# When ScalarE's tables are called up: tiny unread activations where stages begin, and two edits in the mixtures of experts

## The chip, the cores and the metric

The kernel is one program on one core of a Trainium2 chip. Its time is the device time of one execution in microseconds (us); the time of a version is the median of several executions. A profile shows one execution in detail: the span from its first to its last instruction, the instructions of each engine, and what they waited for. The engines are PE (TensorE, the matrix engine; PEld is its loading of weights), DVE (VectorE), ACT (ScalarE), POOL (GpSimd) and SP (SyncE, which here issues most DMA transfers).

## What is computed

Four layers of a Perceiver: 512 tokens of 256 channels (8 sequences of 64) against a context of 8 times 1601 rows of 128 channels. Each layer adds three blocks to the residual `x`: attention to the context, attention or a recurrence over the tokens, and a feed-forward block, which in each of the layers is a mixture of experts.

```python
x = x + _L0_xattn_ref(_layernorm(x, axis=-1), ctx_512, ...)
x = x + _L0_attn_ref(_layernorm(x, axis=-1), ...)
x = x + _L0_ffn_ref(_layernorm(x, axis=-1), ...)
...
x = x + _L3_ffn_ref(_layernorm(x, axis=-1), ...)
```

The parts that matter here are where exponentials and other non-linear functions are taken: softmax (Exp) in all the attentions, `gelu(..., approximate=False)` in the two blocks of layer 0's cross-attention, `silu` in the mixtures of layers 0, 2 and 3, the tanh form of `gelu` in that of layer 1, and in two places of the mixtures:

```python
# layer 0: two of 8 experts, their shares
top_logits, idx = jax.lax.top_k(router, K)
probs = jax.nn.softmax(top_logits.astype(jnp.float32), axis=-1).astype(x.dtype)
...
# layer 3: two of 16 experts, and a shared one behind a gate
shared = shared * jax.nn.sigmoid(x @ shared_gate_w.T)
logits = x @ gate_w.T
probs = jax.nn.softmax(logits.astype(jnp.float32), axis=-1)
rw, sel = jax.lax.top_k(probs, TOP_K)
rw = rw / rw.sum(axis=-1, keepdims=True)
```

## The kernel before

**Layout.** Everything is in 32-bit floats on 128 partitions. The 512 tokens are four tiles of 128 (`NI` = 4); the residual `X` stays on chip throughout. The stages follow one another in program order, each with its own pools of on-chip buffers. By the trace: a1 and m1 (self-attention of layer 0's cross block and its feed-forward) up to about 120 us; a2 (attention to the context, 16 heads of 32) about 120 to 567; m2 to 610; b0 (attention over tokens) to 663; f0 (first mixture) to 775; x1 (context attention) to 828; r1 (recurrence) to 868; f1 (second mixture) to 971; x2 (context attention, heads of 64) to about 1410; b2 to 1475; f2 (third mixture) to 1560; x3 (context attention, 16 heads of 16, "narrow") to about 1850; b3 to 1923; f3 (fourth mixture) to the end.

**What sets the order.** Each engine works through its own queue strictly in order and waits there on semaphores. Inside `tc.manual_schedule(...)` blocks (`flash` of x1, `turned_attention` of a2, x2 and x3, m1's feed-forward, and the loops over experts) the order of the named engines is the order in which the program is written. Outside of them a scheduler orders each engine's instructions from estimated times: what is ready first goes first, and of what is ready, what is written first. `tc.keep_in_program_order(...)` pins one instruction behind whatever was traced before it on its engine. All waits are placed by the framework. ScalarE's functions come from tables; the framework puts an instruction `ACT_TABLE_LOAD` ahead of an activation whose function is not in the tables that are loaded at that point of ACT's final order.

**The context attentions.** In a2, x2 and x3 `turned_attention` runs 7 steps for each of 16 halves (a sequence and half of its heads). A step makes scores of 256 context rows on PE into `psS` (L883; x3: L1006), copies them out on ACT into `raw` (L884; x3: L1011), keeps a running maximum on DVE (`top`, L799 and L805), subtracts the maximum nine to ten steps later on DVE (`raw`, L826), takes Exp on ACT (L830), and sums values on PE (`psav`, L895; x3: L1025). The score buffers are two (x3: one large one), so PE's next scores wait for ACT's copies. In x1 `flash` works on 8 half tiles: scores (L1710), their maximum on DVE (L683 to L688, `nm`), Exp on ACT (`P`, L696), transposes (`psp`, L710), sums (L1716).

**The mixtures.** A routing chain of small operations on DVE (`top2`, `chosen`, `deal`: lines 1108 to 1228) finds each token's two experts and its place. Indirect DMAs on POOL (L1217) then deal the rows out in that order, SP reads them back (L1239), and a hand-ordered loop runs the experts' tiles. Meanwhile PE makes the shared expert's halves in `up(c)` (L1144), whose Silu is on ACT (`sg`, L1147) and whose product is on DVE (`hT`, L1148). In f3, `softmax_e` (lines 1091 to 1098) stands at the head of the routing chain: the maximum (`gm`), the subtraction (`sc`, L1092), Exp on ACT (L1093), the sum (`gs`, L1095) and the division. Its gate is the sigmoid of column 16 of the logits (L2098), read only by the sums at the end of the stage. In f0 the two shares need one Exp, `e2` (L1656), written after the last `up`, and three small DVE operations (`r` and `e2`, lines 1658 to 1660); they are read at the end of the stage by `collect`.

**Where stages begin.** m1, f0, x1, f1, x2 and others open with `keep_busy(ps, n)`: n matmuls on `ones` (L349) whose result nobody reads. `transposed` and `lin_T` then turn the normalised tokens and make queries; copies out of them alternate between ACT (L340) and DVE (L342) in `evac`. `turn_into` (L1330) is an Identity activation on ACT. `collect` (L1301) fetches half of the answered rows through a DMA queue of ACT's own.

Of the kernel before, what the change touches and what calls it, by code (L numbers as in the profile page):

```python
# [11 lines left out]
F32 = mybir.dt.float32  # L12
AF = mybir.ActivationFunctionType
# [260 lines left out]
def perceiver(ctx: ExitStack, tc: tile.TileContext, d, col_at, row_at, const_at, out):  # L274
# [46 lines left out]
    def chunks(w, n):  # L321
        return w.rearrange("p (k n) -> p k n", n=n)
# [14 lines left out]
    def evac(dst, src):  # L337
        turn[0] ^= 1
        if turn[0]:
            nc.scalar.copy(dst, src)  # L340
        else:
            nc.vector.tensor_copy(dst, src)  # L342

    def keep_busy(ps, n):

# [1004 lines left out]
    with tc.tile_pool(name="l0res", bufs=1) as res, ExitStack() as both:  # L1350
# [82 lines left out]
        with general() as ps, tc.tile_pool(name="m1", bufs=1) as mp:  # L1433
# [30 lines left out]
            def turn2(i):  # L1464
                if i >= 0:
                    turn_into(ps, xT2, i, xn[:, i, :], ("a2lnx_g", "a2lnx_b"))

            keep_busy(ps, 8)
            staggered(norm1, enter1)
            with tc.manual_schedule(engines=FOUR):  # L1470
# [13 lines left out]
        with tc.tile_pool(name="a2o", bufs=1) as op:  # L1484

            qT = op.tile([P, 4, NT], F32, tag="qT", name="qT")
            with ExitStack() as _:
                wq, wk, wv, li1 = (weight("a2" + k) for k in ("wq", "wk", "wv", "li1"))
                wk3, wv3 = chunks(wk, CY), chunks(wv, P)
                with general() as ps:  # L1490
                    lin_T(ps, chunks(wq, 512), xT2, 512, lambda c, t: evac(qT[:, c, :], t))
                ps, psS, psO, fp = turned_pools("a2")
                with ps as ps, psS as psS, psO as psO, fp as fp:
# [55 lines left out]
                        psS, psO, fp, lambda b: qks[b].rearrange("p h s -> p (h s)"), lambda b: (cns[b], cts[b]), leave  # L1549
                    )  # L1550
                    turned_attention(ps, fp, *parts, hooks)
            with general() as ps, tc.tile_pool(name="m2", bufs=1) as mp:
                x3 = tpool.tile([P, C // P, NT], F32, tag="T", name="T")
                xn = nat.tile([P, NI, C], F32, tag="nat", name="xn")
                mvs2 = {}

                def scale2(i):
                    norm_by(xn[:, i, :], xo[:, i, :], mvs2[i])
                    nc.gpsimd.tensor_tensor(X[:, i, :], X[:, i, :], xo[:, i, :], ALU.add)

                def enter2(i):
                    turn_into(ps, x3, i, xn[:, i, :], ("a2ln3_g", "a2ln3_b"))

                def attended(i, t):
                    nc.vector.tensor_tensor(xo[:, i, :], t, xo[:, i, :], ALU.add)
                    mvs2[i] = norm_of(xo[:, i, :])
                    if i > 0:
                        scale2(i - 1)
                    if i > 1:
                        enter2(i - 2)  # L1570

                lin_nat(ps, chunks(li1, C), qT, attended)
                keep_busy(ps, 2)
                enter2(NI - 2)
                scale2(NI - 1)
                keep_busy(ps, 3)
                enter2(NI - 1)
                after_attention("a2", xo, x3, mp, ps, into_X, lambda: None)
# [60 lines left out]
    with general() as ps, tc.tile_pool(name="f0", bufs=2) as pool:  # L1639
# [5 lines left out]
        xT = transposed(ps, xn)  # L1645
        lg = logits(ps, pool, wg, xT)
        hots, (m1, m2) = top2(pool, lg, 8)
        sel = chosen(pool, hots, 8)
        up, down = gated_parts(ps, pool, xT, ws1, ws2, 704)
        up(0)  # L1650
        ofi, n = deal(ps, pool, dealts[0], xn, hots, sel, 8, W0)
        for c in range(1, 6):
            up(c)
        e2 = pool.tile([P, NI], F32, tag="e2", name="e2")
        nc.vector.tensor_tensor(e2, m2, m1, ALU.subtract)
        nc.scalar.activation(e2, e2, AF.Exp)  # L1656
        r = pool.tile([P, NI], F32, tag="pr", name="pr")
        nc.vector.tensor_scalar(r, e2, 1.0, None, ALU.add)
        nc.vector.reciprocal(r, r)
# [16 lines left out]
    with tc.tile_pool(name="x1", bufs=1) as pool:  # L1676
# [5 lines left out]
        qb = pool.tile([P, NI], F32, tag="qb", name="qb")  # L1682
        oT = pool.tile([P, NT], F32, tag="oT", name="oT")
        with general() as ps:
            keep_busy(ps, 7)
            xT = transposed(ps, normed(X))
            lin_T(ps, wq, xT, C, lambda c, t: nc.scalar.activation(qT[:, c, :], t, AF.Identity, bias=col("x1bq", c)))
            lin_T(ps, wk, qT, CY, lambda c, t: evac(qk, t))
            t = ps.tile([P, 512], F32, tag="ps", name="psb")
            for i in range(NI):  # L1690
                for k in range(2):
                    nc.tensor.matmul(t[:, i : i + 1], qT[:, k, i * P : (i + 1) * P], col("x1bk", k), start=k == 0, stop=k == 1)
            nc.vector.tensor_copy(qb, t[:, :NI])
# [142 lines left out]
    with general() as ps, tc.tile_pool(name="f1", bufs=2) as pool:  # L1836
# [3 lines left out]
        xn = normed(X)  # L1840
        xT = transposed(ps, xn)
        sc = softmax_e(pool, logits(ps, pool, wg, xT), 8)
        hots, _ = top2(pool, sc, 8)
        sel = pool.tile([P, NI, 8], F32, tag="sel", name="sel")
        nc.vector.tensor_tensor(sel, hots[0], hots[1], ALU.add)
# [74 lines left out]
    with tc.tile_pool(name="x2", bufs=1) as pool:  # L1920
# [2 lines left out]
        qT = pool.tile([P, 8, NT], F32, tag="qT", name="qT")  # L1923

        with general() as ps:
            keep_busy(ps, 2)
            xT = transposed(ps, normed(X))
            lin_T(ps, chunks(wq, 1024), xT, 1024, lambda c, t: evac(qT[:, c, :], t))
            add_row_to_X("x2o")
# [117 lines left out]
    with tc.tile_pool(name="x3", bufs=1) as pool:  # L2047
        wq, wkv, wo = (weight("x3" + k) for k in ("q", "kv", "o"))
        qT = pool.tile([P, 2, NT], F32, tag="qT", name="qT")
        oT = pool.tile([P, 2, NT], F32, tag="oTall", name="oTall")  # L2050
        with general() as ps:
            xT = transposed(ps, normed(X))
            lin_T(ps, chunks(wq, C), xT, C, lambda c, t: evac(qT[:, c, :], t))
        ps, psS, psO, fp = turned_pools("x3", 1, 1, 3)
# [20 lines left out]
    with general() as ps, tc.tile_pool(name="f3", bufs=2) as pool:  # L2075
# [3 lines left out]
        xT = transposed(ps, xn)  # L2079
        lg = logits(ps, pool, wg, xT)  # L2080
        sc = softmax_e(pool, lg[:, :, :16], 16)
        hots, (m1, m2) = top2(pool, sc, 16)
        sel = chosen(pool, hots, 16)
        up, down = gated_parts(ps, pool, xT, ws1, ws2, 704)
# [9 lines left out]
        for k, m in enumerate((m1, m2)):  # L2094
            shares.append(pool.tile([P, NI], F32, tag=f"share{k}", name="share"))
            nc.vector.tensor_tensor(shares[k], m, r, ALU.mult)
        gate = pool.tile([P, NI], F32, tag="gate", name="gate")
        nc.scalar.activation(gate, lg[:, :, 16], AF.Sigmoid)  # L2098

        def act(t, h, ys):  # L2100
            sg = pool.tile([P, P], F32, tag="sgd", name="sgd", bufs=2)
# [31 lines left out]
```

## Time and profile before

| what | us |
| --- | --- |
| three runs | 2009.70, 2011.72, 2015.39 |
| median | 2011.72 |
| the profiled execution | 2014.61 |
| its span, first to last instruction | 2012.8 |
| ACT busy in it | 1036.5 (1721 instructions) |
| mean granted clock of PE, as a share of full speed | 0.984 |

The profile's groups give, for a line, engine and operation, the tiles written and read, the count, the busy time, the mean time of one, and after the second bar the idle time of the engine just ahead of them with what ended it. The timeline gives the start and length of instructions in order of time, with the idle time ahead and its releaser in brackets. PE's instructions overlap, so an idle of PE is the time in which none ran. In the first page's slices of the span the granted clock of PE is printed in tenths; a table by stretches gives it as a share, with the busy time of each engine.

### The profile page before, as it was taken

What the parts mean: (1) busy time and instruction counts of PE and PEld (TensorE: products, weight loads), DVE (VectorE), ACT (ScalarE), POOL (GpSimd) and SP (SyncE); (2) the same over time, 40 slices, a digit from 0 to 9 for tenths busy, and PEclk for the clock granted to TensorE, in tenths of its full rate; (3) what the DMA queues carried; (4) which work ended last, traced back from release to release, by engine and by line L of the source; (5) the groups of instructions that cost most, each with busy time, mean ns of one, the idle gap of its engine ahead of it and who ended that gap; (6) DMA issues with size and microseconds to landing.
All of it is one profiled execution on the core that took longest, in us unless ns stands there. A gap on an engine that the chain in (4) does not pass through costs nothing.

```text
span 2012.8 us, 36872 instructions
## 1 busy us (share of the span) xinstructions
PE 1894.9 (94%) x15394; PEld 1411.5 (70%) x15394; DVE 1235.7 (61%) x2124; ACT 1036.5 (51%) x1721; POOL 270.0 (13%) x331
## 2 busy tenths in 40 slices
PE   8989999999999998989999999999999799998899
PEld 6656777777768576669567777778866577776757
DVE  6556676766726433661366666665544599999743
ACT  2347777777532222402265555654212599998323
POOL 3431010111012211000000000000122210100124
PEclk8999999999999999999999999999999899999999
DMA  9310000000005207318200100100421110100322
GB/s 312 117 63 1 18 18 18 18 28 1 1 26 221 89 27 270 118 62 277 100 17 34 34 34 34 35 18 17 183 82 61 48 35 19 36 19 17 143 76 98
DMA packets 38230, 142.29 MB, mean 71 GB/s; under 512 B 4936, under 2 KB 17872, under 8 KB 32496
## 3 DMA queue, kind: packets, MB, share of 16 engines
q1 hardware_dynamic: 32448, 127.98, 17.8%
q0 software_dynamic: 3696, 10.11, 1.4%
q8 instruction: 122, 2.00, 0.4%
q10 hardware_dynamic: 1920, 1.84, 0.3%
q14 instruction: 44, 0.36, 0.1%
HBM read 129.28 MB, written 19.71 MB: 74 GB/s over the span
## 4 chain that ended last, share of the span: by engine, by line
PE 64%; DVE 15%; ACT 9%; issue 2%; POOL 2%; DMA 2%; SPq 0%; DVEq 0%; ACTq 0%; POOLq 0%
PE psav L895 17%; PE psS L883 16%; PE psgd L1260 4%; DVE raw L826 4%; DVE top L805 4%; PE psl L412 2%; PE psn L421 2%; PE psy L1281 2%; ACT raw L1011 2%; ACT raw L830 1%; PE psh L1903 1%; PE psy L1907 1%; PE psg L1144 1%; PE psq L471 1%; ACT cn L1413 1%
## 5 line engine op out<-in xcount | busy, mean ns | idle before, releaser
L895 PEld LDWEIGHTS psav<-cn,raw 128*128 128x128 f32 (+1 forms) x3328 | 403.2, 192 | 87.6 <-issue 86.3
L826 DVE TENSOR_TENSOR raw<-raw,mb 128x1024 f32<-128x1024 f32 (+1 forms) x336 | 381.7, 1140 | 62.5 <-ACT mb L822 62.5
L895 PE MATMUL psav<-cn,raw 128*128 128x129 f32 (+1 forms) x3328 | 407.4, 275 | 0.7 <-ACT raw L830 0.7
L883 PE MATMUL psS<-qk,ct 128*128 128x512 f32 (+1 forms) x832 | 397.5, 600 | 8.3 <-ACT raw L884 8.3
L805 DVE TENSOR_TENSOR top<-raw,top 128x1024 f32<-128x1024 f32 (+1 forms) x240 | 267.8, 1116 | 137.1 <-ACT raw L884 113.5
L830 ACT ACTIVATE raw<-raw 128x1024 f32<-128x1024 f32 (+1 forms) x336 | 334.6, 998 | 14.4 <-DVE raw L826 12.0
L884 ACT COPY raw<-psS 128x512 f32<-128x512 f32 (+1 forms) x416 | 235.7, 584 | 133.1 <-PE psS L883 129.7
L883 PEld LDWEIGHTS psS<-qk,ct 128*128 128x128 f32 (+1 forms) x832 | 138.2, 187 | 115.6 <-issue 80.9
L349 PE MATMUL busy<-ones 128*128 128x256 f32 x444 | 108.9, 389 | 6.1 <-DVE X L1306 3.0
L1011 ACT COPY raw<-psS 128x1024 f32<-128x1024 f32 (+1 forms) x112 | 106.5, 951 | 4.9 <-PE psS L1006 4.9
L1006 PE MATMUL psS<-qz,kT 32*128 32x128 f32 (+1 forms) x1664 | 78.0, 298 | 22.5 <-ACT raw L1011 22.3
L349 PEld LDWEIGHTS busy<-ones 128*128 128x128 f32 x444 | 82.3, 194 | 20.7 <-issue 4.1
L1260 PE MATMUL psgd<-w,xdT 128*128 x272 | 90.3, 463 | 1.4 <-DVE xdT L1249 1.4
L485 POOL MEMSET vz<- 128x528 f32 (+1 forms) x12 | 7.4, 642 | 612.2 <-PE pso L1961 428.2
L1006 PEld LDWEIGHTS psS<-qz,kT 32*128 32x128 f32 (+1 forms) x1664 | 55.6, 183 | 46.4 <-ACT raw L1011 38.3
L799 DVE TENSOR_TENSOR top<-raw 128x1024 f32<-128x1024 f32 x48 | 58.7, 1222 | 47.6 <-ACT raw L884 36.4
L361 POOL TENSOR_TENSOR mv<-mv,mhalf 128x1 f32<-128x1 f32 x76 | 42.9, 569 | 323.3 <-DVE mv L360 311.7
L1025 PE MATMUL psav<-raw,v 128*32 128x64 f32 (+1 forms) x3328 | 72.5, 228 | 3.4 <-ACT raw L830 1.7
L1025 PEld LDWEIGHTS psav<-raw,v 128*32 128x32 f32 (+1 forms) x3328 | 54.0, 113 | 18.5 <-issue 3.5
L822 ACT COPY mb<-psmb 128x512 f32<-128x512 f32 x48 | 28.1, 585 | 75.0 <-PE psmb L820 66.9
L992 PEld LDWEIGHTS psv<-w_x3kv_None,ct 128*128 128x128 f32 (+1 forms) x416 | 54.0, 190 | 15.8 <-issue 3.2
L1286 POOL DMA_INDIRECT answered<-rows,homes x53 | 50.9, 960 | 94.8 <-ACT rows L1284 56.2
(425 smaller groups left out, 2762.0 us busy)
## 6 DMA issues: line engine op xcount, KB each, us to landing
cn<-in_cn_dram SPq DMA_DIRECT2D x24, 838.5 KB, 4.6
ct<-in_ct_dram SPq DMA_DIRECT2D x24, 800.5 KB, 5.3
dealt<-in_deal_dram SPq DMA_DIRECT2D x3, 2955.5 KB, 26.5
w<-in_f0w_dram SPq DMA_DIRECT2D x8, 1088.0 KB, 14.5
w_f1up<-in_f1up_dram SPq DMA_DIRECT2D x8, 1024.0 KB, 4.9
w_f1dn<-in_f1dn_dram SPq DMA_DIRECT2D x8, 1024.0 KB, 5.5
w<-in_f2w_dram SPq DMA_DIRECT2D x8, 1024.0 KB, 12.6
w<-in_f3w_dram SPq DMA_DIRECT2D x16, 384.0 KB, 8.2
```

Source lines behind the costliest of these rows:

```text
L349: nc.tensor.matmul(t[:, : 2 * P], ones, ones.unsqueeze(1).to_broadcast([P, 2, P]), start=True, stop=True)
L799: nc.vector.tensor_tensor(hd["top"], hd["raw", 0], raw, ALU.max)
L805: nc.vector.tensor_tensor(top[:n, :m, :], raw, top[:n, :m, :], ALU.max)
L826: nc.vector.tensor_tensor(raw, raw, halves[h]["mb"][:n].unsqueeze(1).to_broadcast([n, m, 512]), ALU.add)
L830: nc.scalar.activation(raw, raw, AF.Exp)
L883: nc.tensor.matmul(x[:n], ct[:, kt * P : kt * P + n], qk, start=True, stop=True)
L884: nc.scalar.copy(raw[:n, i, :], x[:n])
L895: nc.tensor.matmul(oa[:, j // 2, j % 2 * CO : (j % 2 + 1) * CO], w[:n, i, j * P : (j + 1) * P], cn[:n, kt, :], start=kt == 0 and j % 2 == ...
L1006: nc.tensor.matmul(x[:n, g, i * P : (i + 1) * P], kTs[h][r, kt * P : kt * P + n], qzs[b][r, c].rearrange("p m s -> p (m s)"), start=True, ...
L1011: nc.scalar.copy(raw[:n, :m, :].rearrange("p i (g s) -> p i g s", g=4), x[:n, :, : m * P].rearrange("p g (i s) -> p i g s", s=P))
L1025: nc.tensor.matmul(oa[32 * g : 32 * g + 32, s * S : (s + 1) * S], vs[h % 2][:n, 4 * kt + g, 2 * s : 2 * s + 2, :].rearrange("p s d -> p (s ...
L1260: nc.tensor.matmul(y[:, :m], st[t]["xT"][:, k, :], w[:, bass.ds(x + at + k * m, m)], start=k == 0, stop=k == C // P - 1)
```

## The change

A helper `prepare(f)` takes one column of `ones` through function `f` on ACT into a tile of one column that nobody reads, and pins it behind what was traced before it on ACT. It is called seven times: with Gelu in m1 and m2, with Exp ahead of a2's queries and at the head of x1, x2 and x3, and with the tanh form of Gelu in f1 just behind the softmax. In f0 the difference of the two best logits and its Exp are written ahead of `chosen` and of all `up` calls. In f3 the gate is no longer a Sigmoid: it is Exp of the negated logit, held below 1e36, plus one, and the reciprocal of that, written right behind `softmax_e`.

```diff
--- before.py
+++ after.py
@@ -340,6 +340,11 @@
             nc.scalar.copy(dst, src)
         else:
             nc.vector.tensor_copy(dst, src)
+
+    def prepare(f):
+
+        x = small.tile([P, 1], F32, tag="warm", name="warm", bufs=1)
+        tc.keep_in_program_order(nc.scalar.activation(x, ones[:, 0:1], f))
 
     def keep_busy(ps, n):
 
@@ -1465,6 +1470,7 @@
                 if i >= 0:
                     turn_into(ps, xT2, i, xn[:, i, :], ("a2lnx_g", "a2lnx_b"))
 
+            prepare(AF.Gelu)
             keep_busy(ps, 8)
             staggered(norm1, enter1)
             with tc.manual_schedule(engines=FOUR):
@@ -1487,6 +1493,7 @@
             with ExitStack() as _:
                 wq, wk, wv, li1 = (weight("a2" + k) for k in ("wq", "wk", "wv", "li1"))
                 wk3, wv3 = chunks(wk, CY), chunks(wv, P)
+                prepare(AF.Exp)
                 with general() as ps:
                     lin_T(ps, chunks(wq, 512), xT2, 512, lambda c, t: evac(qT[:, c, :], t))
                 ps, psS, psO, fp = turned_pools("a2")
@@ -1549,6 +1556,7 @@
                         psS, psO, fp, lambda b: qks[b].rearrange("p h s -> p (h s)"), lambda b: (cns[b], cts[b]), leave
                     )
                     turned_attention(ps, fp, *parts, hooks)
+            prepare(AF.Gelu)
             with general() as ps, tc.tile_pool(name="m2", bufs=1) as mp:
                 x3 = tpool.tile([P, C // P, NT], F32, tag="T", name="T")
                 xn = nat.tile([P, NI, C], F32, tag="nat", name="xn")
@@ -1645,15 +1653,15 @@
         xT = transposed(ps, xn)
         lg = logits(ps, pool, wg, xT)
         hots, (m1, m2) = top2(pool, lg, 8)
+        e2 = pool.tile([P, NI], F32, tag="e2", name="e2")
+        nc.vector.tensor_tensor(e2, m2, m1, ALU.subtract)
+        nc.scalar.activation(e2, e2, AF.Exp)
         sel = chosen(pool, hots, 8)
         up, down = gated_parts(ps, pool, xT, ws1, ws2, 704)
         up(0)
         ofi, n = deal(ps, pool, dealts[0], xn, hots, sel, 8, W0)
         for c in range(1, 6):
             up(c)
-        e2 = pool.tile([P, NI], F32, tag="e2", name="e2")
-        nc.vector.tensor_tensor(e2, m2, m1, ALU.subtract)
-        nc.scalar.activation(e2, e2, AF.Exp)
         r = pool.tile([P, NI], F32, tag="pr", name="pr")
         nc.vector.tensor_scalar(r, e2, 1.0, None, ALU.add)
         nc.vector.reciprocal(r, r)
@@ -1682,6 +1690,7 @@
         qb = pool.tile([P, NI], F32, tag="qb", name="qb")
         oT = pool.tile([P, NT], F32, tag="oT", name="oT")
         with general() as ps:
+            prepare(AF.Exp)
             keep_busy(ps, 7)
             xT = transposed(ps, normed(X))
             lin_T(ps, wq, xT, C, lambda c, t: nc.scalar.activation(qT[:, c, :], t, AF.Identity, bias=col("x1bq", c)))
@@ -1840,6 +1849,7 @@
         xn = normed(X)
         xT = transposed(ps, xn)
         sc = softmax_e(pool, logits(ps, pool, wg, xT), 8)
+        prepare(AF.Gelu_apprx_tanh)
         hots, _ = top2(pool, sc, 8)
         sel = pool.tile([P, NI, 8], F32, tag="sel", name="sel")
         nc.vector.tensor_tensor(sel, hots[0], hots[1], ALU.add)
@@ -1923,6 +1933,7 @@
         qT = pool.tile([P, 8, NT], F32, tag="qT", name="qT")
 
         with general() as ps:
+            prepare(AF.Exp)
             keep_busy(ps, 2)
             xT = transposed(ps, normed(X))
             lin_T(ps, chunks(wq, 1024), xT, 1024, lambda c, t: evac(qT[:, c, :], t))
@@ -2049,6 +2060,7 @@
         qT = pool.tile([P, 2, NT], F32, tag="qT", name="qT")
         oT = pool.tile([P, 2, NT], F32, tag="oTall", name="oTall")
         with general() as ps:
+            prepare(AF.Exp)
             xT = transposed(ps, normed(X))
             lin_T(ps, chunks(wq, C), xT, C, lambda c, t: evac(qT[:, c, :], t))
         ps, psS, psO, fp = turned_pools("x3", 1, 1, 3)
@@ -2079,6 +2091,11 @@
         xT = transposed(ps, xn)
         lg = logits(ps, pool, wg, xT)
         sc = softmax_e(pool, lg[:, :, :16], 16)
+
+        gate = pool.tile([P, NI], F32, tag="gate", name="gate")
+        nc.scalar.activation(gate, lg[:, :, 16], AF.Exp, scale=-1.0)
+        nc.vector.tensor_scalar(gate, gate, 1.0e36, 1.0, ALU.min, ALU.add)
+        nc.vector.reciprocal(gate, gate)
         hots, (m1, m2) = top2(pool, sc, 16)
         sel = chosen(pool, hots, 16)
         up, down = gated_parts(ps, pool, xT, ws1, ws2, 704)
@@ -2094,8 +2111,6 @@
         for k, m in enumerate((m1, m2)):
             shares.append(pool.tile([P, NI], F32, tag=f"share{k}", name="share"))
             nc.vector.tensor_tensor(shares[k], m, r, ALU.mult)
-        gate = pool.tile([P, NI], F32, tag="gate", name="gate")
-        nc.scalar.activation(gate, lg[:, :, 16], AF.Sigmoid)
 
         def act(t, h, ys):
             sg = pool.tile([P, P], F32, tag="sgd", name="sgd", bufs=2)
```

## The prediction, as it was put on record

> **What bounds the kernel now.** I read the page's busy shares and its chain first, then the groups of ScalarE (ACT) with their forms apart, then the timeline around every table load, engine by engine.
>
> ```profile
> PE 1894.9 (94%) x15394; PEld 1411.5 (70%) x15394; DVE 1235.7 (61%) x2124; ACT 1036.5 (51%) x1721; POOL 270.0 (13%) x331
> ...
> PE 64%; DVE 15%; ACT 9%; issue 2%; POOL 2%; DMA 2%; SPq 0%; DVEq 0%; ACTq 0%; POOLq 0%
> ```
>
> TensorE (PE) holds 64% of the chain that ends last, ACT 9%. So a microsecond of ACT counts only where PE or VectorE (DVE) stands still for it. The loads are these:
>
> ```profile
> L830 ACT ACT_TABLE_LOAD x3 | 3.8, 1283 | 0.1
> L1147 ACT ACT_TABLE_LOAD x3 | 3.8, 1283 | 0.1
> ...
> L1346 ACT ACT_TABLE_LOAD x2 | 2.6, 1283 | 1.8 <-PE psl L412 1.8
> ...
> L696 ACT ACT_TABLE_LOAD x1 | 1.3, 1283 | 4.9 <-DMA cn<-in_cn_dram 4.9
> ```
>
> With one each at L638, L528, L1656, L1904, L1150, L2098 and L1093 that is 16 loads of 1.283 us, 20.5 us, 1.0% of the span. Each stands before the first Exp, Gelu, Silu or Sigmoid that follows one of another kind; copies and Identity never bring one. The question is which are waited for.
>
> **The four loads that PE waits for.** In the second attention of layer 0 (a2):
>
> ```profile
> 158.54 0.76 ACT L1504 ACTIVATE ct<-psc,cols 128x512 f32<-128x512 f32 x1
> 159.32 1.28 ACT L830 ACT_TABLE_LOAD   x1
> 160.61 1.06 ACT L830 ACTIVATE raw<-raw 128x1024 f32<-128x1024 f32 x1
> ...
> 162.19 3.03 PE L883 MATMUL psS<-qk,ct 128*128 128x512 f32 x4 [3.13 <-ACT raw L884]
> ```
>
> ACT has no gap from 156.51 to 165.8 us, and PE idles 3.13 us until the copies behind the exponential free its score buffers. The shift that the exponential needs (L826) ended at 155.03. Without the load everything on ACT moves up by 160.61 - 159.32 = **1.29 us**, and PE's idle falls to 1.84. PE is busy 417.2 of the 430 us from 135 to 565, so the shift reaches the end of the stage.
>
> In x1 the first exponential waits for its maximum, then for the load:
>
> ```profile
> 793.03 1.28 ACT L696 ACT_TABLE_LOAD   x1 [4.91 <-DMA cn<-in_cn_dram]
> 794.33 1.75 ACT L696 ACTIVATE P<-psS,nm 128x896 f32<-128x896 f32 x2
> ...
> 795.39 2.00 PE L1710 MATMUL psS<-ct,qk 128*64 128x512 f32 x8 [2.89 <-ACT P L696]
> ```
>
> The DMA named is not the cause: ACT's wait ends at 792.85, where DVE's nm (L686, 792.54 + 0.27) ends. If it is the cause after all, its landing at 793.05 costs 0.02. The load is worth 794.33 - 793.03 = **1.30 us**; the second maximum (793.65 + 0.27 = 793.92) is ready as the second exponential comes up at about 794.0.
>
> In x2 and x3 the a2 pattern returns:
>
> ```profile
> 1013.43 1.28 ACT L830 ACT_TABLE_LOAD   x1
> ...
> 1016.31 1.99 PE L883 MATMUL psS<-qk,ct 128*128 128x512 f32 x4 [1.72 <-ACT raw L884]
> ...
> 1600.38 1.28 ACT L830 ACT_TABLE_LOAD   x1
> ...
> 1603.69 1.24 PE L1006 MATMUL psS<-qz,kT 32*128 32x128 f32 x16 [1.67 <-ACT raw L1011]
> ```
>
> x2: **1.30 us** (1014.73 - 1013.43), inside PE's idle of 1.72. DVE limits the next exponential to 0.78 us earlier (its shift ends at 1015.81 either way), but PE, busy without a break from 1016.31, needs that one only 3.5 us later. x3: 1.29 us at the exponential, and PE's idle of 1.67 takes it; the next exponential gains 0.73, since DVE's second shift ends at 1602.76. Bounds 0.7 to 1.3; I take **1.29**, as PE runs on without a gap from 1603.69 and hands its earlier start on.
>
> **Where the loads go instead.** Seven tiny activations of one column are added. The nearest rows are 128x2 and 128x4 activations of 0.20 and 0.21 us, so each brings 1.28 + 0.21 = 1.49 us of ACT. Each is pinned behind what is traced before it on ACT and reads `ones`, written at the start, so it waits for nothing. Idle ACT that takes them: 6.6 us before 83.11 (m1); 9.7 before 575.52 (m2); 11.6 after the collecting DMAs of 768.73 (x1); 18.1 before 896.90 (f1); 17.3 before 976.02 (x2); 14.7 after the DMAs of 1555.49 (x3). Only a2 is tight: the last `turn_into` ends at 120.12, the first copy of qT starts at 122.23, idle 2.11 against 1.49, 0.6 to spare. Were the cover gone, a2 would lose at most the 1.29 it gains. The two DMAs on ACT's queue stay ahead of the x1 and x3 activations; nothing moves past SP's or POOL's queue.
>
> **Loads that nobody waits for: nothing.** The Gelu loads at 87.78 and 581.81 are caught up before lin_T ends: PE makes a chunk every 1.72 us, ACT takes 0.69 for one and waits 1.03 from the third on (the second time from the first on). At 899.22 PE is in psh until 902.15 and psy follows without a gap.
>
> **First mixture (f0): nothing.** Moving e2's Exp ahead of the Silus removes two loads (678.60, 680.12) and puts the Silu load behind an Exp that is ready at about 676.85: first sg about 678.35 instead of 677.99. But its hT waits for psu until 680.07, and the next sg waited 1.43 us for PE. On DVE the subtraction of 0.15 already ran at 676.66, between steps of the routing; the three operations of r (0.15 to 0.16 each) at most leave the placing chain, whose rows land at 700.23, a us before PE asks at 701.30. Bounds -0.4 to +0.4.
>
> **Fourth mixture (f3).**
>
> ```profile
> 1930.30 0.21 ACT L2098 ACTIVATE gate<-lg 128x4 f32<-128x4 f32 x1 [0.79 <-DVE lg L1082]
> 1930.52 1.28 ACT L1093 ACT_TABLE_LOAD   x1
> 1931.82 0.26 ACT L1093 ACTIVATE sc<-sc 128x64 f32<-128x64 f32 x1
> ...
> 1932.11 0.22 DVE L1095 TENSOR_REDUCE gs<-sc 128x4 f32<-128x64 f32 x1 [1.33 <-ACT sc L1093]
> ```
>
> Sigmoid ran ahead of the softmax and cost it a load. DVE's subtraction starts at 1930.55 and gs at 1932.11, 1.56 us apart. The same pair in f1, with no load between, is 878.24 and 878.81: 0.57, or some 0.62 at twice the width. Gain **0.94**, on the chain: PE idles 2.13 us before 1936.52 for `sel`, and is busy from there. The gate's two new DVE operations (nearest rows L1658 0.15, L1659 0.16) fit in DVE's 0.4 us wait for the exponential; outside it they cost about 0.35. So 0.6 to 0.94, and I take 0.94.
>
> **Sum without the clock:** 1.29 + 1.30 + 1.30 + 1.29 + 0.94 = **6.1 us**; low end 0.7 for x3, 0.6 for f3, a2 at nothing: 3.9.
>
> **The clock.** Three of these waits are followed by half clock:
>
> ```profile
> 163.00:166.40 3.40, 3.40 (x10) 2.06 (x9) 2.55 (x3) 2.69 (x5) 0.00 (x0) 0.50 0.00 0
> ...
> 1603.40:1610.20 6.80, 6.51 (x105) 5.50 (x105) 4.72 (x4) 5.19 (x8) 0.00 (x0) 0.50 0.01 2
> ...
> 1937.90:1941.30 3.40, 3.40 (x5) 1.35 (x5) 2.54 (x13) 0.15 (x1) 0.00 (x0) 0.50 0.00 0
> ```
>
> (After the stretch: busy us of PE, PEld, DVE, ACT, POOL, then PEclk.) PE at half speed for 3.4 us loses 1.7. The idle ahead shrinks from 3.13 to 1.84, 1.67 to 0.38 and 2.13 to 1.19. Idle of 1.72 (x2) and 2.89 (x1) brought no half clock, so the edge is not sharp. If all three go: 1.7 + 1.5 + 1.7 = 4.9 us more, x3's share held to 1.5 by DVE, which waits 1.88 there at 1610.28. If new ones come elsewhere: -1.7 each. I take **1.1**, under a quarter of 4.9. The Trainium skill ("TensorE: Matmul & The Clock Gate", The HAM clock gate) tells of free-running windows of 3413 ns whose activity sets the clock; the stretches of 3.4 and 6.8 us agree. By that, a wait leads to half clock by chance of position, and shorter waits do so more rarely.
>
> **Total:** 6.1 + 1.1 = 7.2 us. The profiled execution took 2014.61 (span 2012.8, 1.8 around it), 2.9 above the median of 2011.72 (2009.7 to 2015.39). The terms are waits of one pass, so they come off either: 2007.4 for that execution, **2004.5** from the median, 0.36% less. What a measurement can tell from no change is about 0.3%, 6.0 us: faster means under 2005.7, slower above 2017.7.
>
> **Rivals.**
> 1. *Half the gain stays hidden* (0.13): a2's load lands in front of a qT copy, and in x3 the gain ends at DVE, whose L826 and L805 are 55% of the chain from 1625 to 1845. Then 1.30 + 1.30 + 0.7 + 0.6 = 3.9: 2007.8, "same". Against: PE's idle names ACT at each place.
> 2. *The clock goes with the waits* (0.17 with the next): 6.1 + 4.9 = 11.0: 2000.7. For: half clock follows three of five. Against: x1 and x2 idle as long without it. A switch may also cost more than its row: the load at 672.74 follows a copy that ended at 672.72, and the exponential at 160.61 a load that ended at 160.60, so I give 0.02 to a cost that the rows hide; were it as long again as the load, four exposed loads give 4 x 1.28 = 5.1 more, 1999.4. The Trainium skill ("ScalarE: Activation LUTs", What ACT_TABLE_LOAD costs) has about 1.38 us of drain beside the 1283 ns; the row agrees on the load and shows no drain.
> 3. *The order comes out otherwise* (0.05): outside the hand-ordered blocks a scheduler decides, and a tiny activation could sink to the first real one. Then the loads stay, f3 alone gains 0.94, seven activations cost 7 x 0.21 = 1.5: 2012.3, "same".
> 4. *Slower* (0.07): the new column lies in a pool that stays for the whole kernel and moves later tiles. Place: the matmuls of L895 and L883, 407.4 + 397.5 = 805 us and nearly all of two PE-bound loops. It ends slower than before from 6.1 / 805 = 0.8% on them, and slower by over 0.3% from 1.5%: at 2%, 16.1 - 6.1 gives 2021.7. For: like matmuls of L895 differ by 1% now (272 to 275 ns). Against: nothing shows that addresses set it.
>
> **How the numbers follow.** The forecast has 0.58, of which three quarters lie beyond 6.0 us: 0.44, and 0.17 from rival 2 make faster 0.61; the last quarter, with rivals 1 and 3, same 0.32; slower 0.07. The range runs from 1999.5 (rival 2) to 2010.5 (rival 1's 2007.8 with one new half-clock stretch of 1.7 and 1.0 for the spread of a median); rivals 3 and 4 stay outside.
>
> **What would show it.** 12 table loads instead of 16, seven of them before an added activation, none at L2098, L1656 or before the first L830 of a stage. PE's idle before the named L883, L1710 and L1006 shorter by 1.3 each. From DVE's subtraction to gs in f3 about 0.6. No half clock after at least one of the three waits. Wrong if the four attention stages do not shorten, or if L340 qT starts later than before.

## The result and the profile after

| | before | after |
| --- | --- | --- |
| median, us | 2012.53 (15 runs, 2009.44 to 2018.52) | 2004.68 (15 runs, 2001.61 to 2014.78) |
| ratio to before | 1 | 0.9955, 95% interval 0.9942 to 0.9968 |
| profiled execution, us (its span) | 2014.61 (2012.8) | 2003.5 (2001.7) |
| mean granted clock of PE in it | 0.984 | 0.989 |
| table loads | 16 | 14 |

The kernel became faster: 0.45% by the ratio on record, and 7.85 us (0.39%) between the two medians, where 7.2 us (0.36%) was forecast. The page's busy row and chain by engine, of the kernel after:

```profile
PE 1885.7 (94%) x15394; PEld 1404.1 (70%) x15394; DVE 1235.7 (62%) x2126; ACT 1034.7 (52%) x1726; POOL 271.0 (14%) x331
...
PE 62%; DVE 16%; ACT 9%; issue 3%; DMA 2%; POOL 2%; SPq 0%; DVEq 0%; ACTq 0%; POOLq 0%
```

PE runs the same 15394 matmuls in the same order, 9.2 us shorter in sum: part of the difference between these two executions is PE's clock. (The profiled execution is a good one: its clock of 0.989 stands against a mean of 0.985 over the 15 runs.) The order being the same, the two traces can be laid side by side matmul by matmul; wherever the difference of the start times steps, something was won or lost.

**a2, x2, x3: won, in x3 in part.** ACT's timeline of the kernel after, where the table is called up and where the first exponential of a2 runs, and PE's next scores:

```profile
119.34 0.81 ACT L1335 ACTIVATE T<-pst,cols 128x128 f32<-128x128 f32 x2 [2.58 <-PE pst L1333]
120.17 1.28 ACT L347 ACT_TABLE_LOAD   x1
121.46 0.20 ACT L347 ACTIVATE warm<-ones 128x1 f32<-128x1 f32 x1
122.27 0.59 ACT L340 COPY qT<-psl 128x512 f32<-128x512 f32 x1 [0.60 <-ACT warm L347]
...
158.35 0.76 ACT L1511 ACTIVATE ct<-psc,cols 128x512 f32<-128x512 f32 x1
159.01 1.04 ACT L835 ACTIVATE raw<-raw 128x1024 f32<-128x1024 f32 x1
...
160.58 1.98 PE L888 MATMUL psS<-qk,ct 128*128 128x512 f32 x4 [1.71 <-ACT raw L889]
```

The load and its activation lie in the gap before the first copy of qT, which still comes 0.60 us after them. The first exponential starts 0.66 us after `ct` does, not 2.07 as before: **1.41 us**, not 1.29. The load took 1.283 and 0.03 of gaps ahead of it and behind it, and it also kept the exponential from starting 0.10 us before `ct` had ended, as it does now. PE's idle falls from 3.13 to 1.71. In x2, x3 and ahead of f3's positions, PE's timeline after:

```profile
1007.98 1.98 PE L888 MATMUL psS<-qk,ct 128*128 128x512 f32 x4 [0.30 <-ACT raw L889]
...
1591.06 0.73 PE L1011 MATMUL psS<-qz,kT 32*128 32x128 f32 x16 [0.26 <-ACT raw L1016]
...
1594.04 0.73 PE L1011 MATMUL psS<-qz,kT 32*128 32x128 f32 x16 [0.58 <-ACT raw L1016]
...
1926.03 0.42 PE L1192 MATMUL pspos<-sel,const 128*128 128x80 f32 x2 [0.49 <-DVE sel L1181]
```

The first idles of x2 and x3 and that of f3 were 1.72, 1.67 and 2.13: 1.42, 1.41 and 1.64 less (in f3 PE itself came late here, in a half-clock stretch). In a2 and x2 the matmuls keep the lead to the end of the stage. In x3 they don't keep all of it: at the next scores PE stands again, 0.58 us, which it did not do before. ACT's timeline there, after:

```profile
1591.64 1.06 ACT L835 ACTIVATE raw<-raw 128x1024 f32<-128x1024 f32 x1 [0.63 <-DVE raw L831]
```

The second exponential now waits 0.63 us for DVE's subtraction, and PE's scores wait for the copy behind it. Before, PE ran at half clock from 1603.40 to 1610.20 and came to these scores too late to wait. At full clock it would have reached them at 1606.09, 2.40 us after 1603.69 as it does now, and the copy (which started at 1604.99, and 1.06 us later lets PE go) would have released it at 1606.05; so of the 1.41 an estimated 1.41 - 0.58 = **0.83** is left, and the rest of what x3 shows between the two profiles is the clock.

**x1: won and given back.** ACT, PE and SP's queue in x1, after:

```profile
785.68 2.00 ACT L701 ACTIVATE P<-psS,nm 128x896 f32<-128x896 f32 x2 [4.95 <-DMA cn<-in_cn_dram]
...
786.74 1.07 PE L1719 MATMUL psS<-ct,qk 128*64 128x512 f32 x2 [1.61 <-ACT P L701]
788.72 1.72 PE L1719 MATMUL psS<-ct,qk 128*64 128x512 f32 x6 [0.91 <-DMA ct<-in_ct_dram]
...
772.17 0.48 SPq L1710 DMA_DIRECT2D cn<-in_cn_dram  x1
772.70 13.23 SPq L1712 DMA_DIRECT2D ct<-in_ct_dram  x3
```

The exponential runs at once and PE's idle falls from 2.89 to 1.61. Two matmuls later PE stands again, for 0.91 us: the fourth `ct`, issued at 772.70, lands 16.0 us later at 788.7. The step is -1.28 us at the first of these matmuls, and by the third +1.50 us has come back.

**f0: not what was said.** ACT in f0, after:

```profile
663.94 1.28 ACT L1152 ACT_TABLE_LOAD   x1
670.91 0.60 ACT L1152 ACTIVATE sg<-psg 128x512 f32<-128x512 f32 x1 [5.68 <-PE psg L1149]
671.52 1.28 ACT L1658 ACT_TABLE_LOAD   x1
672.82 0.20 ACT L1658 ACTIVATE e<-e 128x4 f32<-128x4 f32 x1
673.04 1.28 ACT L1152 ACT_TABLE_LOAD   x1
675.66 0.60 ACT L1152 ACTIVATE sg<-psg 128x512 f32<-128x512 f32 x1 [1.34 <-PE psg L1149]
```

The scheduler still puts the first Silu ahead of the share's exponential, so both loads stay and there are 14, not 12. Behind the last of them ACT still waits 1.34 us for PE, so they cost nothing.

**f3.** DVE and ACT at the softmax, after:

```profile
1918.88 0.17 DVE L2097 TENSOR_SCALAR gate<-gate 128x4 f32<-128x4 f32 x1
1918.96 0.22 DVE L1097 TENSOR_TENSOR sc<-lg,gm 128x64 f32<-128x64 f32 x1
1919.10 0.17 DVE L2098 RECIPROCAL gate<-gate 128x4 f32<-128x4 f32 x1
1919.50 0.22 DVE L1100 TENSOR_REDUCE gs<-sc 128x4 f32<-128x64 f32 x1 [0.24 <-ACT sc L1098]
...
1919.21 0.26 ACT L1098 ACTIVATE sc<-sc 128x64 f32<-128x64 f32 x1 [0.36 <-DVE sc L1097]
1919.49 1.28 ACT L1152 ACT_TABLE_LOAD   x1
```

From the subtraction to `gs` 0.54 us, before 1.56. The gate's reciprocal runs while DVE would wait for the exponential; the load now stands behind the exponential.

**The clock.** Three windows of the kernel after (busy us of PE, PEld, DVE, ACT, POOL, then PEclk):

```profile
163.00:166.40 3.40, 3.40 (x22) 2.44 (x21) 2.76 (x3) 2.55 (x5) 0.00 (x0) 1.00 0.00 0
664.30:671.10 6.80, 6.80 (x20) 4.64 (x20) 2.51 (x14) 1.12 (x2) 0.00 (x0) 0.50 0.23 77
1590.80:1597.60 6.80, 5.96 (x135) 4.76 (x138) 6.59 (x7) 6.11 (x9) 0.00 (x0) 1.00 0.01 2
```

Behind a2's and x3's first exponentials the clock is now full. In f0 it is half for 6.8 us, where before it was half for 3.4. Such stretches come and go between executions, so the experiments below take the mean clock over many runs.

### The profile page after: what moved, and what is told of

Same layout as the page of the kernel before. It is cut to its first block, busy times and chain, and to the rows that moved or that the text cites. A ratio compares the mean times of both kernels' runs of the same rounds, so it can differ in the third digit from the quotient of the medians.

```text
span 2001.7 us, 36879 instructions
## 1 busy us (share of the span) xinstructions
PE 1885.7 (94%) x15394; PEld 1404.1 (70%) x15394; DVE 1235.7 (62%) x2126; ACT 1034.7 (52%) x1726; POOL 271.0 (14%) x331
## 4 chain that ended last, share of the span: by engine, by line
PE 62%; DVE 16%; ACT 9%; issue 3%; DMA 2%; POOL 2%; SPq 0%; DVEq 0%; ACTq 0%; POOLq 0%
PE psav L900 17%; PE psS L888 16%; PE psgd L1265 4%; DVE raw L831 4%; DVE top L810 4%; PE psl L417 2%; PE psy L1286 2%; PE psn L426 2%; ACT raw L1016 2%; ACT raw L835 2%; PE psh L1913 1%; PE psy L1917 1%; ACT cn L1418 1%; PE psS L526 1%; PE psqk L941 1%
## 5 line engine op out<-in xcount | busy, mean ns | idle before, releaser
L900 PEld LDWEIGHTS psav<-cn,raw 128*128 128x128 f32 (+1 forms) x3328 | 402.3, 191 | 87.1 <-issue 85.8
L900 PE MATMUL psav<-cn,raw 128*128 128x129 f32 (+1 forms) x3328 | 406.7, 275 | 0.7 <-ACT raw L835 0.7
L888 PE MATMUL psS<-qk,ct 128*128 128x512 f32 (+1 forms) x832 | 396.2, 598 | 5.5 <-ACT raw L889 5.5
L888 PEld LDWEIGHTS psS<-qk,ct 128*128 128x128 f32 (+1 forms) x832 | 138.1, 187 | 112.6 <-issue 81.0
```

Source lines behind the costliest of these rows:

```text
L888: nc.tensor.matmul(x[:n], ct[:, kt * P : kt * P + n], qk, start=True, stop=True)
L900: nc.tensor.matmul(oa[:, j // 2, j % 2 * CO : (j % 2 + 1) * CO], w[:n, i, j * P : (j + 1) * P], cn[:n, kt, :], start=kt == 0 and j % 2 == ...
```

## The experiments

The table has every kernel run, with the kernel before beside it (78 runs from the three sets of experiments, mean clock 0.9823, with 0.9822 or 0.9823 in each set, mean time 2015.30). The last column is worked out: one slope of time against mean clock, taken from the scatter of the runs within each kernel, for all 198 runs whose clock was recorded (1.32 us less for each 0.001 more), and the distance of each kernel's mean from the kernel before along it, in us, about ±1.0 (±1.4 for 6 or 7 runs). The 15 runs of the kernel before in the table of the result have no clock on record and a lower mean, 2013.60; the changed kernel's -5.8 stands against the 78.

| kernel | median, us (runs) | ratio to before, 95% | mean clock | at equal clock |
| --- | --- | --- | --- | --- |
| changed kernel | 2004.68 (15) | 0.9955 (0.9942 to 0.9968) | 0.9850 | -5.8 |
| exp_only | 2005.65 (6) | 0.9953 (0.9938 to 0.9967) | 0.9852 | -4.9 |
| f3_only | 2011.72 (12) | 0.9985 (0.9972 to 0.9998) | 0.9831 | -1.2 |
| wrong_table | 2014.33 (12) | 0.9994 (0.9979 to 1.0008) | 0.9827 | +0.4 |
| x2_only | 2011.60 (12) | 0.9985 (0.9968 to 1.0003) | 0.9814 | -3.3 |
| a2_x3 | 2008.75 (12) | 0.9970 (0.9952 to 0.9987) | 0.9844 | -3.0 |
| no_x1 | 2005.34 (8) | 0.9958 (0.9942 to 0.9973) | 0.9855 | -6.0 |
| ct_first | 2001.96 (6) | 0.9934 (0.9918 to 0.9950) | 0.9870 | -6.3 |
| ct_no_x1 | 2006.66 (10) | 0.9959 (0.9943 to 0.9975) | 0.9854 | -4.8 |
| pin_ct | 2006.06 (10) | 0.9960 (0.9944 to 0.9976) | 0.9845 | -5.9 |
| f0_fill | 2006.98 (10) | 0.9960 (0.9946 to 0.9974) | 0.9851 | -4.3 |
| ct_fill | 2003.23 (7) | 0.9934 (0.9911 to 0.9957) | 0.9863 | -6.7 |

PE's order is the same in all (f0_fill and ct_fill have more matmuls on `ones`), so each difference can be read stage by stage in the traces.

**1. The four exponentials alone (exp_only).** From the changed kernel, with the calls of m1, m2 and f1 left out and f0's and f3's edits undone:

```diff
-            prepare(AF.Gelu)
...
-            prepare(AF.Gelu)
...
-        prepare(AF.Gelu_apprx_tanh)
...
-        nc.scalar.activation(gate, lg[:, :, 16], AF.Exp, scale=-1.0)
...
+        nc.scalar.activation(gate, lg[:, :, 16], AF.Sigmoid)
```

> The kernel before with the four tiny exponentials alone (a2, x1, x2, x3); the three Gelu calls, the earlier share exponential of f0 and the new gate of f3 are left out, so f3 has its two table loads again. Theory (only loads that PE waits for have a price): in a2, x2 and x3 the matmul that waits for the first exponentials starts as early against its stage as in the changed kernel (PE idle about 1.7, 0.3 and 0.3 us there), m1, m2 and f1 cost nothing more, and f3 has its 1.4 us back: about 1.4 us over the changed kernel, ratio to before about 0.996. Rival (every load drains the engine, hidden or not): putting the three Gelu loads back late costs 1.3 us each or more, so about 4 us over the two that f3 gives, ratio about 0.998.

It is 0.9 us above the changed kernel at equal clock, inside the error, and f3's idle is 2.13 again. Against the changed kernel the matmuls do not step at m2's or f1's late loads at all; in m1 there is a step, and it is a half-clock stretch from 85 to 88 us (the kernel before, whose load is as late, has none there, and f0_fill, whose load is early, has one). The loads that nobody waits for are worth nothing. The idles of x2 and x3 are as said (0.31, 0.26); a2's is 0.63 instead of 1.7, since PE came to it late out of a half-clock stretch.

**2. f3's gate alone (f3_only).** From the kernel before, only the gate's edit of the change.

> The kernel before with f3's gate alone made from the exponential. Theory: DVE's way from the subtraction of the scores' maximum to the weighted sum falls from 1.56 to about 0.54 us, PE's wait ahead of f3's positions falls from 2.1 to about 0.5 us, and 1.4 us comes off the whole: ratio about 0.9993 plus what the clock does. Rival (the two DVE operations of the gate take back what the loads gave): the wait stays at 2.0 us or more, ratio 1.000.

PE ahead of f3's positions, with the gate's edit:

```profile
1941.66 0.42 PE L1192 MATMUL pspos<-sel,const 128*128 128x80 f32 x2 [1.18 <-DVE sel L1181]
```

From `sc` (1936.71) to `gs` (1937.25) it is 0.54. PE's idle falls from 2.13 to 1.18, by **0.95**, and the step there against the kernel before is 0.95 too. The 1.4 that was expected came from the one profile where PE was late; the 0.94 of the forecast was the better number.

**3. The same activations, the wrong table (wrong_table).** In a2, x1, x2 and x3:

```diff
-            prepare(AF.Exp)
+            prepare(AF.Gelu)
```

> The changed kernel with the same tiny activations at the same places, but in a2, x1, x2 and x3 they call Gelu in place of the exponential, so that the table they call up is the wrong one. Theory: the load stands in front of the first exponential again in all four, PE's waits go back to about 3.1, 1.7 and 1.7 us in a2, x2 and x3, x1's second context pair is no longer waited for, and the time goes 4.0 us (a2, x2, x3) above the changed kernel's, ratio to before about 0.998 with f3's part still gained; the clock may add to it. Rival (the gain comes from where the stages fall in the clock's windows, or from the extra instructions): the time stays with the changed kernel's, ratio about 0.9955.

PE in a2 and x2, with the wrong table called up:

```profile
162.93 3.15 PE L888 MATMUL psS<-qk,ct 128*128 128x512 f32 x4 [3.14 <-ACT raw L889]
...
1020.28 1.99 PE L888 MATMUL psS<-qk,ct 128*128 128x512 f32 x4 [1.72 <-ACT raw L889]
```

Both idles are as before the change, x3's is 1.67 again and x1's 2.89, and the kernel is as slow as the kernel before, though every added activation is there. It is the right table that takes these waits away, not the extra instruction or the place of the stages. At equal clock it stands 6.2 us above the changed kernel, 2 more than the first idles of a2, x2 and x3 add up to; that excess is not explained.

**4. x1's transfers (no_x1, ct_first, ct_no_x1).** With and without x1's `prepare(AF.Exp)`, and with its loads in two orders:

```diff
+                cts = [fp.tile([P, M], F32, tag="ct", name="ct", bufs=4) for j in range(2)]
+                for j in range(2):
+                    nc.sync.dma_start(cts[j], d["ct"][2 * i + j])
                 for j in range(2):
                     cn = fp.tile([P, KT, CO], F32, tag="cn", name="cn", bufs=4)
                     nc.sync.dma_start(cn.rearrange("p k c -> p (k c)"), d["cn"][2 * i + j])
-                    ct = fp.tile([P, M], F32, tag="ct", name="ct", bufs=4)
-                    nc.sync.dma_start(ct, d["ct"][2 * i + j])
-                    ctx_of[2 * i + j] = cn, ct
+                    ctx_of[2 * i + j] = cn, cts[j]
```

> The changed kernel with x1's context loads in another order: the two transposed ones (ct), which the scores read, ahead of the two others (cn). Theory (x1's 1.3 us is given back to the late transfer of the second pair's ct): PE's 0.91 us wait at the second pair's scores goes, and x1 ends 1.2 to 1.5 us earlier against its first exponential; ratio to before about 0.995. Rival (all of x1's 13 MB set its pace): the wait moves on to the cn that the sums read, x1 ends at the same time, ratio as the changed kernel's 0.9955.

> The changed kernel without x1's tiny exponential alone. Theory (what x1 gains is given back to the second pair's ct, which lands at 788.7 us whether or not PE is early): PE waits 2.9 us for the first weights P in place of 1.6, no longer for ct, and x1 ends as late against its start as in the changed kernel, within 0.3 us. Rival (the gain is there and only the clock hides it): x1 is 1.3 us longer from its first scores to its last sums.

> Both at once: x1's ct loads ahead of the cn loads, and no tiny exponential in x1. Theory: with ct on time the load has its price again, so that x1 is 1.3 us longer here than with the new order of loads and the tiny exponential; and the new order alone, against the changed kernel without the tiny exponential, gives only about 0.3 us. Rival (the new order gives its 1.6 us by itself, whatever ScalarE does): x1 is as short as with both.

PE at the second pair's scores, first without the tiny exponential, then with it and `ct` first:

```profile
788.11 1.72 PE L1718 MATMUL psS<-ct,qk 128*64 128x512 f32 x8 [2.89 <-ACT P L701]
```

```profile
787.12 1.72 PE L1720 MATMUL psS<-ct,qk 128*64 128x512 f32 x8 [1.61 <-ACT P L701]
```

From x1's first scores to its output products (each start read from PE's trace):

| | `cn` and `ct` in turn | `ct` first |
| --- | --- | --- |
| load in front of the exponential | 37.15 (before), 37.25 (no_x1) | 39.73 (ct_no_x1), with 6.8 us of half clock |
| table called up early | 37.57 (changed kernel) | 35.75 (ct_first), 36.28 (pin_ct, experiment 5) |

All kernels in this table but ct_no_x1 are without half clock in x1. (The other profiles have some there, and their x1 takes 37.0 to 40.9 us.) In the old order the early table makes x1 no shorter, 0.3 longer if anything. In the new order PE's wait for `ct` is gone and x1 is 1.3 to 1.8 us shorter. In ct_no_x1 the load costs 1.28 at the first exponentials; the wait goes with half clock from 793.5 to 800.3, and against ct_first PE falls another 2.70 us behind there. So how much of the 1.3 to 1.8 the new order gives by itself is not settled by that run. What is shown is that the early table alone gives x1 nothing, because the stall behind the load had hidden a transfer that lands as late either way, and that both edits together do give something.

**5. The exponential of f0 really ahead (pin_ct).** On top of ct_first, `first` being the Silu of an `up`:

```diff
-                nc.scalar.activation(sg[:m], tg[:m], AF.Silu)
+                first = nc.scalar.activation(sg[:m], tg[:m], AF.Silu)
+                if c == 0:
+                    tc.keep_in_program_order(first)
...
-        nc.scalar.activation(e2, e2, AF.Exp)
+        tc.keep_in_program_order(nc.scalar.activation(e2, e2, AF.Exp))
```

> The changed kernel with x1's ct loads first and with f0's share exponential kept ahead of the first Silu on ScalarE by program order (the changed kernel's own order there is Silu, exponential, Silu). Theory: 12 table loads in place of 14, f0 neither faster nor slower by over 0.3 us, since both loads lay in ScalarE's waits for PE; the whole as with the ct order alone, about 2002 us, ratio to before about 0.9935. Rival (a Silu that has to wait for DVE's choice of the best two makes PE wait): f0 0.5 to 2 us longer.

ACT in f0 with both kept in program order:

```profile
671.78 0.20 ACT L1660 ACTIVATE e<-e 128x4 f32<-128x4 f32 x1 [5.40 <-DVE e L1659]
672.00 1.28 ACT L1152 ACT_TABLE_LOAD   x1
673.30 0.60 ACT L1152 ACTIVATE sg<-psg 128x512 f32<-128x512 f32 x1
678.13 0.60 ACT L1152 ACTIVATE sg<-psg 128x512 f32<-128x512 f32 x1 [4.23 <-PE psg L1149]
```

There are 12 loads, and from f0's last transpose to its first expert matmul 33.54 us, as in ct_first (33.54) and the changed kernel (33.53). The two loads were worth nothing, as forecast. The whole came out at 2006.06 instead of about 2002, at a mean clock of 0.9845 against 0.9870: the difference lies in the clock.

**6. Which waits the clock answers to (x2_only, a2_x3).** The kernel before with `prepare(AF.Exp)` in x2 alone, and in a2 and x3 alone.

> The kernel before with x2's tiny exponential alone. Theory (the clock's part belongs to the waits of a2 and x3, behind which half-clock stretches of 3.4 and 6.8 us stood in the profiles with the load exposed, and not to x2's, behind which none stood): x2's wait falls from 1.72 to about 0.3 us, 1.4 us at equal clock, and the mean clock stays at 0.9823 as in the kernel before: about 2013.7 us against its mean of 2015.1. Rival (the clock rises with any wait that goes, or by where the stages fall): the mean clock is 0.9835 or more, or 0.981 and less.

> The kernel before with the tiny exponentials of a2 and x3 alone. Theory: 1.4 us each at equal clock, and the half-clock stretches behind a2's and x3's first exponentials gone, some 10 us at half speed, so that the mean clock goes from 0.9823 to about 0.985: 2.8 us and 3.3 us, a mean of about 2009. Rival (the clock goes by chance or by the kernel's whole length): mean clock at or under 0.9835, a mean of 2011 us or more, and a stretch of half clock still behind x3's first exponential in the profile.

PE in x2, first with x2's alone, then with a2's and x3's:

```profile
1012.34 1.98 PE L888 MATMUL psS<-qk,ct 128*128 128x512 f32 x4 [0.30 <-ACT raw L889]
```

```profile
1013.61 1.98 PE L888 MATMUL psS<-qk,ct 128*128 128x512 f32 x4 [1.72 <-ACT raw L889]
```

The stage does as said in both. The mean clock stays low with x2's alone (0.9814) and rises with the other two (0.9844). Over the whole table, the four kernels whose loads stand in a2 and x3 (before, f3_only, wrong_table, x2_only) have 0.9814 to 0.9831, the nine without them 0.9844 to 0.9870. In the profiles, 6.8 us of half clock follow x3's first exponential in 4 of the 4 with the load there; of the 9 without, one (no_x1) has 3.4 us there and the others have none. In a2 a 3.4 us stretch follows in 2 of 4, and in none of 9; but a2's part is thin, since three of the 9 (exp_only, a2_x3, f0_fill) have 6.8 us just ahead of the exponential where the others have 3.4. x3's stretch alone, 6.8 us at half clock in some 2010, would be 0.0017 of mean clock, an estimate, and the two groups lie some 0.003 apart. x2_only's 3.3 us at equal clock, where 1.4 was expected, shows that the distance at equal clock is good to about 2 us only.

**7. Filling a wait that is no load's (f0_fill, ct_fill).** Nine unread matmuls on the changed kernel, five on ct_first:

```diff
         xT = transposed(ps, xn)
+        keep_busy(ps, 9)
         lg = logits(ps, pool, wg, xT)
```

> The changed kernel with nine more unread matmuls (about 2 us of PE work) in f0 between the transposes and the router's logits, where PE waits 2.15 us for T. No table is touched. Theory (a stretch of PE waiting costs a second time through the clock): the half-clock stretch that begins at f0 in every profile so far (3.4 to 6.8 us long) goes, and f0 is 1.4 us or more shorter from its logits to its positions; the mean clock rises by about 0.001. Rival (the wait isn't what the clock answers to): the half clock stays, and f0 is as long or longer.

> The changed kernel with x1's ct loads first and five unread matmuls in f0 between the transposes and the logits (nine took 4.0 us of PE's time for a wait of 2.2, and put the logits 1.6 us back; five are 2.2 us). Theory: f0's half-clock stretch goes as with nine, now without the delay, so that f0 is 3.3 us shorter from its last transpose to its experts, and x1 1.6 us: a mean of about 2001 us. Rival (a stretch that is filled in one place comes back in another, since the windows of the clock fall otherwise from there on, as with nine): mean clock 0.985 as before it, about 2003 us or more.

PE in f0 with nine, then with five:

```profile
663.86 4.05 PE L354 MATMUL busy<-ones 128*128 128x256 f32 x18
667.74 1.85 PE L1085 MATMUL psg<-w_f0g_None,T 128*128 128x8 f32 x16
```

```profile
664.86 2.32 PE L354 MATMUL busy<-ones 128*128 128x256 f32 x10
667.17 1.95 PE L1085 MATMUL psg<-w_f0g_None,T 128*128 128x8 f32 x16
```

Each call appears as two matmuls of some 0.22 us, so nine took 4.05 us and put the logits 1.58 us back (4.0 after the last transpose instead of 2.42). PE in the same stretch then ran at full clock:

```profile
664.00:667.70 3.70, 3.70 (x19) 3.26 (x18) 0.69 (x1) 3.40 (x4) 0.00 (x0) 1.00 0.00 0
667.70:673.00 5.30, 5.30 (x27) 3.36 (x26) 2.51 (x14) 1.53 (x2) 0.00 (x0) 1.00 0.29 99
```

All eleven profiles without the filling have half clock from f0's logits on or within 3 us of them, for 3.4 or 6.8 us; the two with it have none. From the last transpose to the experts it is 31.67 us with nine and 30.20 with five, 33.53 in the changed kernel (6.8 us of half clock) and 31.89 in the kernel before (3.4). The whole gained nothing that can be measured: the mean clock is 0.9851 against 0.9850, and ct_fill stands with ct_first (both 0.9934). The rival was right there: in f0_fill's profile stretches stand elsewhere instead, 6.8 us of half clock in x1 (788.7) among them, behind a wait of 1.50 us for `ct`.

## Why the prediction came out right, step by step

- **a2, x2 (1.29, 1.30): right, each 0.1 too small.** The first exponential moved by 1.41 us in a2, and PE's idle shrank by 1.42 and 1.42. The row of the load does not show the overlap of neighbouring activations that the load also takes away. The wrong table brought both idles back.
- **x3 (1.29): the wait was right, the size was not.** PE's first idle shrank by 1.41, and 0.58 of it came back at the next scores: 0.83 by the rows, near the lower bound of 0.7. The forecast saw that DVE lets the next exponential gain 0.73 only, but took 1.29 because PE "runs on without a gap from 1603.69". It did so because it ran at half clock there. In 8 of the 9 profiles with x3's table called up early PE has the wait of 0.58; the ninth (no_x1) and the four with the load have half clock at that place and no such wait. So rival 1 was right about x3, where the gain ends at DVE.
- **x1 (1.30): the step that failed.** The forecast followed ACT's wait to its cause on DVE, and that was right: the exponential ran earlier. It did not ask what PE needs two matmuls later. In the profile before, that `ct` was issued at 780.28 and took 15.3 us, to 795.6, and PE reached it at 795.87: 0.3 us of slack, where 1.3 was counted. The stage took 37.57 us, 37.15 before, so by the prediction's own sign one of its four attention stages did not shorten. With x1's activation alone left out (no_x1), nothing that can be measured is lost.
- **f3 (0.94): right.** 0.95 less idle and as large a step with the edit alone. The two DVE operations hid in the wait, as costed.
- **The Gelu loads at nothing: right** (m2, f1: no step; m1: none but a clock stretch).
- **f0 at nothing: right in price, wrong in reason.** The two loads were not removed, because writing an activation earlier does not place it earlier outside the hand-ordered blocks. Rival 3 named this for the tiny activations, which were pinned; it came true for the one that was not. Removed, the loads are still worth nothing (pin_ct).
- **a2's cover held:** qT starts 0.60 us after the tiny activation.
- **The clock (1.1 of 4.9): mis-sized.** The mean clock rose from 0.9823 to 0.9850, which is 3.6 us on the slope of the table; against the 15 runs of the result, whose mean is 1.7 lower than that of the 78, it may be nearer to 2. Of the three stretches counted, a2's and x3's went; in f3 one stands ahead of the positions in the profile after (1917.0 to 1923.8), and one behind them in that of f3_only.
- **Sum.** Without the clock 6.1 was forecast. The rows give 1.42 (a2) + 1.41 (x2) + 0.83 (x3) + 0.95 (f3) - 0.3 (x1) = 4.3, the comparison at equal clock 5.8 ± 1.0 on a slope that is good to about 2 us; where the other 1.5 come from stays open. The 2.1 us that x1 and x3 lack were made up by more clock than was counted, so the total was right partly by luck: errors cancelled. Rival 2 (the clock goes with the waits) holds a part of the truth.
- **Rival 2's second half, a cost that the rows hide, fell.** The price was 1.41, not 2.6, for a load in front of an activation. The Trainium skill ("ScalarE: Activation LUTs", What ACT_TABLE_LOAD costs) has about 1.38 us of drain beside the 1283 ns; the runs show some 0.13 beside the load.
- **Rival 4 fell.** L900 took 406.7 us and L888 396.2, against 407.4 and 397.5.

The best version run is the changed kernel with x1's `ct` loads first: 0.9934 (0.9918 to 0.9950). That it beats the changed kernel is shown inside x1 (1.3 to 1.8 us); in the whole the two intervals overlap, and two other kernels with this order of loads, ct_no_x1 and pin_ct, came out no faster than the changed kernel.

## What to carry to other kernels

Look for table loads whose activation starts right behind them, as it does in a2, x1, x2, x3 and f3 (0.01 us), while another engine waits for that activation; only those have a price, here the load's own 1.28 us and some 0.13 of gaps and lost overlap. Where the activation still has to wait behind its load (0.4 us in m2, 4.0 in f0), the load costs nothing. Idle time ahead of a load is no proof that it is hidden: in x1 ACT stood idle for 4.91 us, and the load came only when that wait was over. A tiny activation in an earlier gap takes the load away. Before counting a stall as a gain, look at everything the next few instructions of the waiting engine need, transfers first: whatever landed during the stall may be the next wait. A stretch that ran without gaps at half clock may have gaps at full clock. Where a scheduler orders an engine, moving a line moves nothing for certain; read the order in the trace or pin it.

## What the runs showed of the hardware that was not expected

- Half-clock stretches go with some waits and not with others of like length: the 1.67 us in x3 went with 6.8 us of half clock in 4 of the 4 profiles that have them, the 1.72 us in x2 in none of the 4 (before, f3_only, wrong_table, a2_x3), and the 2.9 us in x1 in 3 of the 5 (f3_only, wrong_table, ct_no_x1; not before and no_x1).
- The clock spreads the time of one kernel: the changed kernel ran between 2001.61 us (clock 0.987) and 2014.78 (0.980), more than the whole effect of the change.
- A stretch removed by filling one wait (f0) was not a gain of the whole: the mean clock stayed at 0.985.
